# A planned attention kernel: each output store placed behind the landing of the last one, step lengths set from traces, places found anew

## Chip, cores and metric

One core of a Trainium2 chip. The metric is the time of one execution in microseconds (us), median over runs. The kernel before takes 1759.28 us (three runs, 1757.06 to 1759.89). A kernel counts as faster or slower from 2% on. Runs of one call share a chip; the chips of different calls differ, so each experiment below is compared with runs of the kernel before in the same call.

## The reference

A layer of graph attention on 16 batches of 1024 rows of 512 numbers, 8 heads of 64, with one sparse adjacency matrix for all batches:

```python
h = jnp.maximum(_layernorm(x, axis=-1), 0.0)
q, k, v = h @ Wq + bq, h @ Wk + bk, h @ Wv + bv          # in 8 heads of 64
scores = jnp.einsum('bihd,bjhd->bhij', q, k) / jnp.sqrt(64)
scores = scores + mask                                    # -1e9 where adj == 0
weights = softmax(scores); out = jnp.einsum('bhij,bjhd->bihd', weights, v)
return x + out
```

## The kernel before

Rows are sorted by their number of neighbours into 8 tiles of 128. For each tile, GpSimd gathers keys and values of the neighbours, VectorE multiplies with the queries and sums (`multiply`, `score`), ScalarE takes exponents and weighs (`exponent`, `weigh_s`), VectorE and GpSimd add up (`fold`, `join`), GpSimd adds x and stores the rows (`residual`, `put_out`). A batch has 14 such units, and a number behind a step (multiply 12, score 12) is that of its unit in the batch. TensorE meanwhile transposes normalized rows (`flip`), projects keys and values one batch ahead and queries of this batch, and adds up the weighed pieces of some units (`add_up`). For rows with many neighbours it also passes on the sums of their weights (`pass_on`, on the tile `p_more`), which needs a sum from VectorE (`more`). Before the transposes a tile's rows are normalized: VectorE takes statistics (`stats`, `variance`), GpSimd a power (`power`), VectorE a shift (`shift`), and ScalarE applies them (`norm`).

The order of the steps is not written by hand. A planner simulates five engines with a length, a place (priority) and dependences for each step, and each engine then runs its steps strictly in the order that comes out:

```python
def add(self, key, engine, length, place, after=(), uses=(), delay=0.15, moves=0.0):
    self.number[key] = len(self.ops)
    self.ops.append((key, engine, length, place, after, uses, delay, moves))
# ...
add(("residual", b, home), "POOL", 1.42, i + 2.49, [("scale", b, home)], [o, ("x", n)])
add(("put_out", b, home), "POOL", 1.5, i + 0.07, [("residual", b, home)], [("x", n)], delay=4.0, moves=0.75)
# ...
POOLS = dict(x=14, h=2, pht=2, hT=11, pkv=2, kvt=3, q=2, q0=1, g=6, acc=2, o=1)
# ...
def put_out(b, t):
    nc.gpsimd.indirect_dma_start(out=out_rows, out_offset=on(ap=perm[:, t : t + 1], axis=0),
                                 in_=X.pop(b * NT + NT - 1 - t)[:], in_offset=None, element_offset=b * N * D)
```

On the chip a store always waits until the last one has landed, since both write the same tensor. The planner of before does not know that.

## Time and profile before

| | before |
|---|---|
| median of 3 | 1759.28 us |
| profiled execution, span | 1752.1 us |
| TensorE busy / waits | 1618.9 / 122.5 us |
| GpSimd waits for the landing of a store | 37.2 us |

(The waits are the sums of all rows of the waits by engine.) The prediction shows the main views. Two more are needed to see where the time went. The first cuts the execution into start, twelve steady batches, and end. The cuts are the mark F of the prediction (end of TensorE's wait before the transposes of tiles 0/1 of the batch after next) of the first and the last steady batch. Columns: stretch, length, busy time of PE, PEld, DVE, ACT, POOL with counts, granted clock, DMA share, GB/s.

```profile
0.00:301.04 301.04, 264.57 (x740) 125.92 (x740) 251.56 (x446) 215.06 (x714) 214.10 (x219) 0.98 0.76 272
301.04:1546.97 1245.93, 1177.77 (x3121) 546.87 (x3121) 1127.26 (x1285) 1113.74 (x4213) 975.85 (x889) 0.98 0.88 314
1546.97:1752.10 205.13, 176.52 (x436) 79.01 (x436) 179.72 (x193) 160.33 (x631) 140.96 (x129) 0.92 0.77 285
```

The second is VectorE in order of time from multiply 12 on to the mark F at 1235.78 (start, duration, line, operation):

```profile
1229.55 2.29 DVE L876 TENSOR_TENSOR g<-g,pq 128x2048 f32<-128x2048 f32 x1
...
1232.95 0.68 DVE L913 TENSOR_TENSOR g<-g,g 128x512 f32<-128x512 f32 x1
1233.65 1.23 DVE L615 SCALAR_TENSOR_TENSOR shift<-mv,rstd 128x2 f32<-128x2 f32 x1
```

These are multiply 12, then (variance and fold 10 left out) join 9 and the shift that the norms and with them TensorE's transposes wait for. From the start of multiply 12 to F it is 6.23 us. The shift takes 1.23 us for two numbers a row: a GpSimd addition (1233.61, 1.25 us) runs beside it, and without one the shift takes 0.15; that will matter.

### The profile page before, as it was taken

The numbers are of one execution on the slowest core, as the hardware profiler recorded it, in microseconds if no ns is written. First come the engines' busy times: TensorE is split into PE (matmuls) and PEld (weight loads), VectorE is DVE, ScalarE is ACT, GpSimd is POOL, SyncE is SP. The second block draws the span as 40 slices with busy tenths as digits, with TensorE's granted clock in tenths as the row PEclk, the third lists the DMA queues.
The fourth block names the chain that finished last, engine by engine and source line by source line (L and its number), as shares of the span: only waits on it lengthen the run. The fifth ranks groups of instructions, "written<-read, shape, count | busy, mean of one in ns | idle before, by whom it ended". The sixth has DMA issues, their size and how long they took to land.

```text
span 1752.1 us, 19712 instructions
## 1 busy us (share of the span) xinstructions
PE 1618.9 (92%) x4295; PEld 751.8 (43%) x4295; DVE 1558.5 (89%) x1922; ACT 1489.1 (85%) x5556; POOL 1330.9 (76%) x1235
## 2 busy tenths in 40 slices
PE   6979898999999999999999999999999999999796
PEld 3444444444444444444444444444444444444333
DVE  5788989899898979989898998989989898988897
ACT  5359989898898988889898888989899898889965
POOL 4757778787787868877787877878787787877774
PEclk9989999999999999999999999999999999999989
DMA  5388889888898988988898888989988898888894
GB/s 219 132 321 293 309 292 344 309 324 316 287 329 304 339 298 309 323 284 327 305 350 303 304 304 293 346 318 328 322 294 313 293 346 304 318 311 290 310 359 169
DMA packets 150742, 531.73 MB, mean 303 GB/s; under 512 B 19916, under 2 KB 19916, under 8 KB 150616
## 3 DMA queue, kind: packets, MB, share of 16 engines
q0 software_dynamic: 109840, 390.70, 62.5%
q1 hardware_dynamic: 40776, 139.71, 21.7%
q8 instruction: 36, 0.59, 0.1%
q14 instruction: 90, 0.74, 0.1%
HBM read 429.51 MB, written 100.82 MB: 303 GB/s over the span
## 4 chain that ended last, share of the span: by engine, by line
PE 45%; DVE 18%; POOL 8%; ACT 6%; issue 4%; DMA 3%; POOLq 0%; DVEq 0%
PE pq L642 15%; PE pk L642 12%; PE pv L642 8%; DVE g L876 5%; ACT g L902 4%; PE acc L925 4%; DVE g L907 3%; DVE weights L880 3%; PE pht L632 3%; POOL g L866 3%; DVE shift L615 3%; DMA out_dram<-x,perm 2%; POOL x L966 2%; POOL g L907 1%; DVE g L896 1%
## 5 line engine op out<-in xcount | busy, mean ns | idle before, releaser
L902 ACT ACTIVATE g<-g,weights 128x64 f32<-128x64 f32 x4768 | 1180.3, 340 | 3.2 <-DVE weights L889 2.2
L866 POOL DMA_INDIRECT g<-kv,index x608 | 626.1, 1030 | 204.6 <-issue 143.5
L876 DVE TENSOR_TENSOR g<-g,pq 128x1536 f32<-128x1536 f32 (+2 forms) x208 | 389.1, 1872 | 95.4 <-PE pq L642 90.9
L642 PE MATMUL pq<-wq,hT 128*128 128x512 f32 x1024 | 460.3, 592 | 0.0
L642 PE MATMUL pk<-wk,hT 128*128 128x512 f32 x960 | 439.0, 601 | 1.8 <-ACT hT L637 1.7
L642 PE MATMUL pv<-wv,hT 128*128 128x512 f32 x960 | 431.6, 592 | 0.0
L880 DVE TENSOR_REDUCE weights<-g 128x32 f32<-128x2048 f32 (+2 forms) x224 | 423.2, 1890 | 0.6
L907 DVE TENSOR_TENSOR g<-g 128x512 f32<-128x512 f32 (+1 forms) x271 | 281.1, 1038 | 21.9 <-ACT g L902 19.8
L642 PEld LDWEIGHTS pq<-wq,hT 128*128 128x128 f32 x1024 | 194.7, 190 | 228.0 <-issue 224.7
L642 PEld LDWEIGHTS pk<-wk,hT 128*128 128x128 f32 x960 | 185.8, 194 | 212.9 <-issue 206.0
L642 PEld LDWEIGHTS pv<-wv,hT 128*128 128x128 f32 x960 | 182.5, 190 | 205.3 <-issue 201.9
L969 POOL DMA_INDIRECT out_dram<-x,perm x128 | 148.1, 1157 | 79.2 <-DMA out_dram<-x,perm 34.2
L625 ACT ACTIVATE h<-x,shift,rstd 128x512 f32<-128x512 f32 x120 | 91.3, 809 | 91.5 <-DVE shift L615 91.5
L590 POOL DMA_INDIRECT x<-in_x_dram,perm x128 | 135.9, 1062 | 34.9 <-issue 32.4
L907 POOL TENSOR_TENSOR g<-g 128x512 f32<-128x512 f32 x120 | 153.5, 1279 | 10.7 <-DVE g L907 7.2
L632 PE MATMUL pht<-ident,h 128*128 128x128 f32 x512 | 86.2, 308 | 80.2 <-ACT h L625 78.2
L632 PEld LDWEIGHTS pht<-ident,h 128*128 128x128 f32 x512 | 68.3, 158 | 139.5 <-ACT h L625 104.5
L896 DVE TENSOR_TENSOR g<-g,weights 128x512 f32<-128x512 f32 (+1 forms) x134 | 114.5, 855 | 2.2 <-ACT weights L884 1.7
L653 ACT COPY kvt<-pv 128x512 f32<-128x512 f32 x120 | 69.2, 577 | 43.0 <-PE pv L642 43.0
L966 POOL TENSOR_TENSOR x<-x,o 128x512 f32<-128x512 f32 x67 | 86.3, 1288 | 25.0 <-DVE o L957 22.1
L925 PE MATMUL acc<-g,ident 128*128 128x512 f32 x170 | 95.6, 682 | 2.8 <-POOL g L907 2.8
L637 ACT COPY hT<-pht 128x512 f32<-128x512 f32 x128 | 72.1, 575 | 26.9 <-PE pht L632 26.9
(231 smaller groups left out, 1187.0 us busy)
## 6 DMA issues: line engine op xcount, KB each, us to landing
g<-kv SPq DMA_DIRECT2D x128, 512.0 KB
kv<-kvt SPq DMA_DIRECT2D x120, 512.0 KB
g<-kv,index POOLq DMA_INDIRECT x608, 7.2
adj<-in_adj_dram SPq DMA_DIRECT2D x8, 512.0 KB
x_first<-in_x_dram SPq DMA_DIRECT2D x8, 256.0 KB
x<-in_x_dram,perm POOLq DMA_INDIRECT x128, 4.6
out_dram<-x,perm POOLq DMA_INDIRECT x128, 5.0
wk<-in_L_gnn_Wk_dram SPq DMA_DIRECT2D x1, 1024.0 KB
```

Source lines behind the costliest of these rows:

```text
L590: nc.gpsimd.indirect_dma_start(out=X[n][:], out_offset=None, in_=x_rows, in_offset=on(ap=perm[:, t : t + 1], axis=0), element_offset=b * N * D
L632: nc.tensor.transpose(PH[n][:, c, :], hn[:, ts(c, P)], ident)
L642: nc.tensor.matmul(pt, HT[n][:, c, :], W[name][:, c, :], start=False, stop=(c == DC - 1))
L866: nc.gpsimd.indirect_dma_start(out=G[i][:, s].rearrange("p j d -> p (j d)"), out_offset=None, in_=KV[b % len(KV)][:], in_offset=on(ap=inde ...
L876: nc.vector.tensor_tensor(k, k, Q[b, t][:, None, :].to_broadcast([P, count, D]), ALU.mult)
L880: nc.vector.tensor_reduce(weights[:, w, :], heads(G[i][:, :count, 0, :]), AX.X, ALU.add)
L896: nc.vector.tensor_tensor(v, v, own.to_broadcast([P, n, H, HD]), ALU.mult)
L902: nc.scalar.activation(v[:, h, :], v[:, h, :], AF.Identity, scale=weights[:, c + s, h : h + 1])
L907: engine.tensor_tensor(v[:, 0:n], v[:, 0:n], v[:, first : first + n], ALU.add)
L925: nc.tensor.matmul(ACC[b, home], owner_t if t < 0 else ident, v[:, s, :], start=(u == parts_of(home)[0] and s == 0), stop=(u == parts_of(h ...
L966: (nc.vector if shares_in(b, B, t) and b == B - 1 else nc.gpsimd).tensor_tensor(rows, rows, add, ALU.add)
L969: nc.gpsimd.indirect_dma_start(out=out_rows, out_offset=on(ap=perm[:, t : t + 1], axis=0), in_=X.pop(b * NT + NT - 1 - t)[:], in_offset=No ...
```

## The change

The intent: tell the planner that a store lands before the next can start, correct the lengths to what traces show, and search the places again. The core of the diff (some 60 lines of lengths and places, all of this kind, cut):

```diff
-        add(("rank_of", t), ("DVE", "ACT")[t >= NT // 2], 1.25, (-47.51, -44.58)[t >= NT // 2], rows("key"))
+        add(("rank_of", t), ("DVE", "ACT")[t >= NT // 2], 1.25, (-51.98, -50.40)[t >= NT // 2], rows("key"))
 ...
-        add(("tell", t), "POOL", 1.3, -35.76 + 0.3 * t, [("ranks",), ("shift", (t - NT) // 2)] + behind("tell"), delay=2.0)
-        add(("spread", t), "POOL", 1.3, -28.64 + t, [("list_of", t)] + behind("spread"), delay=2.0)
+        add(("tell", t), "POOL", 1.3, -32.06 + 0.3 * t, [("ranks",), ("shift", (t - NT) // 2)] + behind("tell"), delay=2.0)
+        add(("spread", t), "POOL", 1.3, -40.60 + t, [("list_of", t)] + behind("spread"), delay=2.0)
 ...
+    one_by_one = []
     for k in range(units):
         b, u = divmod(k, NU)
+        if b == B - 1:
+            one_by_one = []
 ...
-        add(("score", k), "DVE", 0.15 + 0.533 * count, i - -0.31, [("multiply", k)], [g])
+        add(("score", k), "DVE", 0.1 + 0.533 * count, i - -0.62, [("multiply", k)], [g])
 ...
-            add(("put_out", b, home), "POOL", 1.5, i + 0.07, [("residual", b, home)], [("x", n)], delay=4.0, moves=0.75)
+            add(("put_out", b, home), "POOL", 1.35, i + 0.07, [("residual", b, home)] + one_by_one, [("x", n)], delay=4.0, moves=0.75)
+            one_by_one = [("put_out", b, home)]
```

No arithmetic, tile or buffer changes. Only the order of each engine's steps does.

## The prediction

> **What bounds the kernel now.** I read the page's busy shares first, then the waits by engine, then the chain in order of time, and last the two stretches into which one batch falls. The kernel runs 16 batches; from the third on each engine repeats one list of instructions per batch. No share alone decides:
>
> ```profile
> PE 1618.9 (92%) x4295; PEld 751.8 (43%) x4295; DVE 1558.5 (89%) x1922; ACT 1489.1 (85%) x5556; POOL 1330.9 (76%) x1235
> ...
> DMA  5388889888898988988898888989988898888894
> ```
>
> TensorE, VectorE, ScalarE and the DMA engines are all near nine tenths busy, so the waits must say who loses time. In the time order of TensorE's instructions, only two waits come back in every batch, both in front of transposes of normalized rows:
>
> ```profile
> 1235.78 1.97 PE L632 MATMUL pht<-ident,h 128*128 128x128 f32 x8 [3.96 <-ACT h L625]
> ...
> 1287.81 0.66 PE L632 MATMUL pht<-ident,h 128*128 128x128 f32 x4 [1.33 <-ACT h L625]
> ```
>
> The first is before the transposes of tiles 0 and 1 of the batch after next (I call its end F), the second before those of tile 4. Over 13 batches the second wait averages 1.71 us (1.08 to 2.80). So I cut a batch at these two points and asked for each engine's busy time:
>
> ```profile
> 1132.94:1185.20 52.26, 50.91 (x134) 23.91 (x134) 44.62 (x59) 43.43 (x166) 40.94 (x38) 0.97 0.83 297
> 1185.20:1235.78 50.58, 46.62 (x126) 21.50 (x126) 49.15 (x50) 49.34 (x187) 40.60 (x38) 0.99 0.93 338
> ```
>
> Columns: stretch, its length, busy time of PE, PEld, DVE, ACT, POOL, granted clock, DMA share, GB/s. The first half is TensorE's: 50.9 of 52.3 us. The second half is VectorE's and ScalarE's: 49.15 and 49.34 of 50.58. The first half varies (51.9 to 55.1, mean 53.0 over 13); the second is 50.56 to 50.59 in ten of twelve, 52.1 in two. A batch is 103.8 us, from 12 batches between 301.0 and 1547.0.
>
> The wait that the change is named for is on GpSimd's queue:
>
> ```profile
> POOL out_dram L969 <- DMA out_dram<-x,perm: 34.2, 11, 4.3
> ...
> 1161.48 1.01 POOL L969 DMA_INDIRECT out_dram<-x,perm  x1 [0.17 <-POOL x L966]
> 1162.79 0.97 POOL L866 DMA_INDIRECT g<-kv,index  x1 [0.30 <-issue]
> 1164.06 0.95 POOL L866 DMA_INDIRECT g<-kv,index  x1 [0.30 <-issue]
> 1167.88 1.00 POOL L969 DMA_INDIRECT out_dram<-x,perm  x1 [2.87 <-DMA out_dram<-x,perm]
> ```
>
> (The first line is the waits by engine: total, times, longest; the rest is GpSimd in time order.) Once per batch the store of tile 7 stands two gathers behind the store of the previous batch's tile 0 and waits for it to land, 6.4 us after it was issued. It holds everything behind it. The other seven stores are far enough apart.
>
> **What the Trainium skill says.** "DMA: Bandwidth & Descriptors", section "Two DMAs through the same engine are not ordered", says only the completion semaphore orders two transfers, so the issuing engine must wait for it. The trace agrees that this wait is built in already: the stores write one tensor, and the second waits for the first's landing. The change therefore adds no wait to the machine, only to the plan. "SBUF — State Buffer", "Who interferes with whom", says a DVE instruction with two SBUF inputs contends with a GpSimd instruction that reads SBUF. The trace agrees: a 128x512 fold of VectorE takes 0.68 us alone and 2.40 us beside GpSimd's 1.28 us addition. "TensorE: Matmul & The Clock Gate", "What's actually happening", gives a halved clock after an idle window of about 3.4 us. The trace agrees: after the 3.96 us wait the granted clock is 0.61 for 3.7 us, then 1.00.
>
> **The change part by part.** The arithmetic, the tiles and the buffers stay. The planner gets one more dependence (store after landing of the last store), truer lengths, and new places; so what changes is each engine's order. Comparing the built orders of one steady batch:
>
> GpSimd. One load of x moves into the place between the two gathers and the store of tile 7. It takes 0.98 + 0.30 = 1.3 us that was waited before, so the wait falls from about 3 to about 1.7 us. The load was formerly after the store, so GpSimd gains 1.3 us per batch.
>
> TensorE, first half (F to tile 4). The sum of the last pieces (one pair of 128x512 matmuls, 0.86 us) and the small pass-on (0.12 us) move in front of the first wait, where TensorE is idle. Two query projections of tiles 7 and 6 come first, the keys of tile 0 later. What is left between F and tile 4: transposes 1.97, twelve projections at 3.65 (0.22 + 3.43 in the chain), three sums at 0.86, two transposes at 0.44: 1.97 + 43.8 + 2.6 + 0.9 = 49.2 us. The same sum for the old order gives 50.7, and 1287.81 - 1.33 - 1235.78 = 50.70 was measured, so the counting holds. The slow clock after the wait now falls on a projection: some 1.7 us at half speed, 0.85 lost, gives 50.05; other clock losses add 0.6 (mean of 13 is 51.3 against 50.7). So 50.7.
>
> Does anything hold tile 4's transposes then? They need tile 4's norm, it needs the shift on VectorE, that the power on GpSimd. On the old path this was GpSimd's chain, store wait included: power at 1283.69, F + 47.9. Now the last sums and hence the gathers and stores behind them come some 2.8 us earlier (third sum at F + 18 instead of F + 21), plus the 1.3: power near F + 44. VectorE reaches the shift near F + 47, since it waits for queries of tiles 5, 4 and 3 (ends near F + 22.8, 26.9, 38.3, plus the clock's 0.85). So the 1.71 us wait vanishes and the first half falls from 53.0 to 50.7: -2.3 us.
>
> Second half. Between the multiply of tile 2 and the shift of the batch after next, the old VectorE list has 42 steps of the plan, the new one the same 42 and three more: a 128x2048 score (2.19 us from start to start), a scale (0.60) and the sum of the pieces' weights (0.13): +2.9 us. VectorE had only 1.1 us of waits there, for ScalarE. ScalarE likewise gets one more weighing of eight 128x64 instructions (1.92) and one exponent (0.12): +2.0. Both were full, so this does lengthen the half. I choose 2.9 less the 1.1 of waits, taken to be absorbed: +1.8 us.
>
> Per batch: -2.3 + 1.8 = -0.5; for 13 batches -6.5 us.
>
> Start. Building the slot lists (88.5 to 92.4, 3.9 us) moves from VectorE's solid stretch 74 to 103 into its waits of 2.84 and 5.39 us for permutation and long rows: -3.9. Statistics of three more tiles (0.85 each) come earlier, +2.5, but leave later; the scatters of permutation data are mixed with the lists' scatters and come up to 3 us later, hidden mostly by the 5.39. TensorE waits for ranks earlier and ends the first eight tiles later, using up its 7.77 us wait. Net -2.
>
> Tail. One fold on GpSimd (1664.62, ready about 1653.4 when VectorE's fold ended) moves ahead of nine gathers. TensorE's 5.89 us wait on it goes, but VectorE, 92.9% busy from 1600 to 1700, sets the pace: -3.
>
> Sum: -11.5 us of 1759.3, so 1748.
>
> **The rivals.** First, the store wait was all of it: 34.2 us over 11 batches and some 9 more under other names. If removing it moved the end by that much, some 40 us would go, 1719. For it: it lies on the chain in several batches. Against: 1.7 us of it stays, and the second half is unmoved by it. Second, the second half takes the full 2.9 and the slow clock or VectorE's waits eat the first half's gain: then 0 to +1 per batch, 1754 to 1770. For it: 97% busy of two engines and a DMA share of 0.93. Third, VectorE's stretched instructions change with the neighbours on GpSimd. In the second half its fold, weighing and shift lose near 4.4 us (2.40 for 0.68, 1.78 for 0.68, 1.75 for 1.22, 1.23 for 0.15). If the new order avoids half, -2.2 per batch more, 1719; if it adds as much, 1777. I cannot see this from an order and set it at nothing.
>
> **Range and chances.** A microsecond per batch is 13 us; I give the halves' difference an error of about 1 us and start and tail together 5 us: 1730 to 1765 for 8 in 10. Faster by over 2% needs 1724 or less, 2.7 us per batch: 0.08. Slower by over 2% (1794.5) needs +2.7 where I have -0.5: 0.02.
>
> **What would show it.** Right: cut at the same two transposes, the first half near 50.7 with no wait before tile 4; the second near 52.6; the wait before tiles 0 and 1 at 4 to 5 us, still on ScalarE's norm; VectorE waiting over 3 us for queries in the first half; store waits near 1.7 us each. Wrong: the wait before tile 4 stays (then GpSimd's chain was not shortened), or the second half stays near 50.6 (then what I call full was not), or a new wait on gathers shows in VectorE.

## The result

The changed kernel takes 1772.24 us (four runs, 1768.43 to 1774.40); in the same rounds the kernel before takes 1759.07. The ratio is 1.0074 with an interval of 1.0055 to 1.0094: within 2%, but slower, and above the predicted range of 1730 to 1765. (A ratio is the mean time of one kernel's fast runs over that of the other's of the same rounds, so it is not quite the ratio of the medians quoted.) A repetition on another chip gave 1769.98 against 1757.08, ratio 1.0075.

The page's busy times of the changed kernel:

```profile
PE 1633.0 (92%) x4232; PEld 763.3 (43%) x4295; DVE 1556.6 (88%) x1922; ACT 1493.1 (84%) x5556; POOL 1348.5 (76%) x1235
```

VectorE and ScalarE do what they did; TensorE is busy 14.1 us longer. (63 of its records, all of small matmuls that add a bias, are missing from this trace; loads of weights show all 4295, so the number of matmuls is the same.)

The stretches cut as above:

```profile
0.00:310.65 310.65, 268.08 (x734) 129.98 (x743) 252.69 (x449) 217.36 (x723) 217.59 (x221) 0.96 0.75 267
310.65:1562.27 1251.62, 1188.24 (x3073) 554.00 (x3121) 1126.59 (x1285) 1117.41 (x4213) 992.05 (x888) 0.96 0.88 312
1562.27:1770.50 208.23, 176.69 (x426) 79.32 (x432) 177.34 (x190) 158.31 (x622) 138.88 (x126) 0.91 0.76 277
```

The start grew by 9.6 us, the twelve batches by 5.7 (104.30 us each instead of 103.83), the end by 3.1; the spans differ by 18.4. The profiled execution of before took 1753.89 us, less than its four timed runs, so this is more than the 13 us between the medians. The second pair of profiles gives 5.2, 7.5 and 3.0, together 15.7.

One steady batch of the changed kernel in its two halves, second half first:

```profile
1195.45:1249.25 53.80, 48.95 (x129) 22.41 (x129) 52.69 (x53) 50.25 (x192) 43.02 (x39) 0.96 0.94 330
1249.25:1298.84 49.59, 49.48 (x128) 23.56 (x131) 39.88 (x55) 42.83 (x161) 39.17 (x35) 0.97 0.84 299
```

Over all batches, the first half fell from a mean of 53.03 us to 50.2 (49.56 to 51.07), as predicted. The second grew from a mean of 50.83 to 54.08. In it VectorE is busy 52.69 of 53.80 us, three instructions and 3.5 us more than in the 50.58 us of before; its idle time only fell from 1.4 to 1.1.

TensorE at these points:

```profile
1246.09 0.60 PE L947 MATMUL p_more<-more,owner_t 128*128 128x8 f32 x2 [4.09 <-DVE more L943]
1246.54 2.05 PE L930 MATMUL acc<-g,ident 128*128 128x512 f32 x2
1249.25 1.97 PE L637 MATMUL pht<-ident,h 128*128 128x128 f32 x8 [0.66 <-ACT h L630]
```

The transposes of tile 4, at 1298.84, have no wait any more. But pass_on (`p_more`) now waits for `more`, here 4.09 us, in every batch, ahead of add_up and the transposes. And what follows this gap at once is slow: the two matmuls of add_up take 2.05 us instead of 1.10 at full clock, eight transposes 1.97 instead of 1.04.

VectorE from multiply 12 on:

```profile
1239.10 2.27 DVE L881 TENSOR_TENSOR g<-g,pq 128x2048 f32<-128x2048 f32 x1
...
1243.24 1.94 DVE L918 TENSOR_TENSOR g<-g,g 128x512 f32<-128x512 f32 x1
1245.10 0.15 DVE L613 TENSOR_SCALAR rstd<-mv 128x2 f32<-128x2 f32 x1
1245.21 0.69 DVE L962 TENSOR_TENSOR o<-g,inv 128x512 f32<-128x512 f32 x1
1245.82 0.21 DVE L943 TENSOR_REDUCE more<-weights 128x8 f32<-128x40 f32 x1
1245.95 2.28 DVE L885 TENSOR_REDUCE weights<-g 128x32 f32<-128x2048 f32 x1
1248.15 0.15 DVE L620 SCALAR_TENSOR_TENSOR shift<-mv,rstd 128x2 f32<-128x2 f32 x1
```

Fold 10 and the statistics of tile 1 are left out at the dots. From multiply 12 to F it is now 10.15 us instead of 6.23: 3.92 more, and the stretch ahead of multiply 12 is 0.7 shorter (43.65 against 44.35). The 3.92, counted from start to start: score 12 2.20, scale 0.61, `more` 0.13, the statistics of tile 1 0.81 (before, they stood ahead of multiply 12), join 9 1.16 more since it now runs beside GpSimd (1.86 against 0.70), the shift 1.09 less since it no longer does (0.06 against 1.15). That is 3.82; small differences make the other 0.1. The statistics only moved within the half: their 0.81 is given back in the 0.7 ahead of multiply 12. What lengthened the half is thus mostly the three added steps, 2.94 us.

GpSimd's waits for the landing of a store:

```profile
POOL x L595 <- DMA out_dram<-x,perm: 27.4, 13, 2.9
...
POOL out_dram L974 <- DMA out_dram<-x,perm: 4.2, 2, 2.6
```

The load of x that moved ahead of the store waits for the very landing that the store waited for: with 14 buffers for x it needs the one that this store frees. All rows for this landing sum to 32.2 us, 37.2 before (33.3 and 30.2 in the second pair). The wait was renamed, not filled.

### The profile page after: what moved, and what is told of

Same layout as the page of the kernel before. It is cut to its first block, busy times and chain, and to the rows that moved or that the text cites. A ratio compares the mean times of both kernels' runs of the same rounds, so it can differ in the third digit from the quotient of the medians.

```text
span 1770.5 us, 19619 instructions
## 1 busy us (share of the span) xinstructions
PE 1633.0 (92%) x4232; PEld 763.3 (43%) x4295; DVE 1556.6 (88%) x1922; ACT 1493.1 (84%) x5556; POOL 1348.5 (76%) x1235
## 4 chain that ended last, share of the span: by engine, by line
PE 47%; DVE 32%; issue 8%; POOL 5%; DMA 4%; ACT 3%; SPq 0%; DVEq 0%; POOLq 0%; ACTq 0%
PE pq L647 19%; PE pk L647 10%; PE pv L647 9%; DVE weights L885 9%; DVE g L881 8%; DVE g L912 6%; PE acc L930 4%; POOL g L871 3%; DMA g<-kv,index 3%; PE pht L637 3%; DVE g L918 2%; ACT g L907 2%; DVE st L604 1%; PE pq L645 1%; DVE g L901 1%
## 5 line engine op out<-in xcount | busy, mean ns | idle before, releaser
L871 POOL DMA_INDIRECT g<-kv,index x608 | 639.0, 1051 | 199.3 <-issue 162.2
L647 PE MATMUL pq<-wq,hT 128*128 128x512 f32 x1024 | 474.4, 607 | 0.2
L647 PE MATMUL pk<-wk,hT 128*128 128x512 f32 x960 | 431.6, 592 | 1.4
L647 PEld LDWEIGHTS pq<-wq,hT 128*128 128x128 f32 x1024 | 202.5, 198 | 229.5 <-issue 224.2
L647 PEld LDWEIGHTS pv<-wv,hT 128*128 128x128 f32 x960 | 182.6, 190 | 209.4 <-issue 206.1
L595 POOL DMA_INDIRECT x<-in_x_dram,perm x128 | 149.2, 1166 | 65.9 <-issue 32.2
L974 POOL DMA_INDIRECT out_dram<-x,perm x128 | 139.4, 1089 | 37.0 <-issue 16.8
L901 DVE TENSOR_TENSOR g<-g,weights 128x512 f32<-128x512 f32 (+1 forms) x134 | 153.9, 1157 | 0.5 <-ACT weights L889 0.5
L658 ACT COPY kvt<-pk 128x512 f32<-128x512 f32 x120 | 69.2, 577 | 71.6 <-PE pk L647 67.6
L889 ACT ACTIVATE weights<-weights 128x32 f32<-128x32 f32 (+2 forms) x224 | 49.4, 220 | 87.2 <-DVE weights L885 86.9
L930 PE MATMUL acc<-g,ident 128*128 128x512 f32 x170 | 101.6, 718 | 17.7 <-POOL g L912 15.1
L637 PEld LDWEIGHTS pht<-ident,h 128*128 128x128 f32 x512 | 70.7, 161 | 67.2 <-ACT h L630 32.2
L637 PE MATMUL pht<-ident,h 128*128 128x128 f32 x512 | 83.5, 309 | 10.5 <-ACT h L630 9.5
```

Source lines behind the costliest of these rows:

```text
L595: nc.gpsimd.indirect_dma_start(out=X[n][:], out_offset=None, in_=x_rows, in_offset=on(ap=perm[:, t : t + 1], axis=0), element_offset=b * N * D
L637: nc.tensor.transpose(PH[n][:, c, :], hn[:, ts(c, P)], ident)
L647: nc.tensor.matmul(pt, HT[n][:, c, :], W[name][:, c, :], start=False, stop=(c == DC - 1))
L871: nc.gpsimd.indirect_dma_start(out=G[i][:, s].rearrange("p j d -> p (j d)"), out_offset=None, in_=KV[b % len(KV)][:], in_offset=on(ap=inde ...
L901: nc.vector.tensor_tensor(v, v, own.to_broadcast([P, n, H, HD]), ALU.mult)
L930: nc.tensor.matmul(ACC[b, home], owner_t if t < 0 else ident, v[:, s, :], start=(u == parts_of(home)[0] and s == 0), stop=(u == parts_of(h ...
```

## The experiments

Eighteen runs in five calls. In the first and the fourth call the kernel before took 1806 and 1792 us instead of 1754 to 1759. All eight profiles of these two calls show waits that no work on the core ends, and none of the other twelve profiles does. The largest such row, from `dep_only`, on the queue of direct transfers (total, times, longest):

```profile
SPq L670 <- remote: 47.2, 3, 17.7
```

So times of these two calls are compared within the call only and with care; the form of their traces is used. What such waits are, and whether it is the chip or something else at work at that time, stays open.

In all edits that place single steps, the finished order is edited by a function `moved`, with `put(step, before= or after=)`.

### The two parts of the change, each alone

`dep_only` is the kernel before with the dependence (the lines with `one_by_one` above), old lengths and places. `no_dep` is the changed kernel without it:

```diff
-            add(("put_out", b, home), "POOL", 1.35, i + 0.07, [("residual", b, home)] + one_by_one, [("x", n)], delay=4.0, moves=0.75)
+            add(("put_out", b, home), "POOL", 1.35, i + 0.07, [("residual", b, home)], [("x", n)], delay=4.0, moves=0.75)
```

> The kernel before with only the new dependence of each output store on the landing of the last one; old lengths and places. Its plan comes out anew: the start keeps its old order (shift -4 ahead of all degree steps), but in each batch score 12 and scale 1 now stand in DVE's order ahead of the shift of tiles 0/1. Theory (what costs is what lies ahead of the shifts): first transposes on TensorE at about 15 us as before, the wait before the transposes of tiles 0/1 later by 2 to 3 us a batch, 1755 to 1790 us, start to the first such wait within 2 us of before's 301.0. Rival (the dependence itself costs or gains, through the order in which stores and loads of x reach the queue): GpSimd's waits for the landing of a store fall by more than half from 69 us in all, and the time falls to 1720 to 1750.

> The changed kernel without the new dependence: only lengths and places. Shift -4 still stands behind degree 2 at the start, and score 12 and scale 1 still ahead of the shift of tiles 0/1. Theory (lengths and places lose it): start to the first wait before transposes of tiles 0/1 still near 310 us, second halves near 54 us, 1765 to 1780 us. Rival (the dependence is what loses): back to 1750 to 1762 us, second halves near 51 us.

On the chip with waits from outside: `dep_only` 1899.75 us, `no_dep` 1808.85, before 1806.29, ratios 1.0532 and 1.0021. Both were run again on a quiet chip:

> The kernel before with the new dependence alone, a second time. Theory (an order of steps made for old lengths, in which TensorE waits 140 us for transposes, is bad on any chip): 1870 us or more again, whatever the kernel before takes. Rival (its 5.3% were due to that chip): below 1800 us on a chip where the kernel before takes 1757.

> The changed kernel without the new dependence, a second time, for a chip on which the kernel before takes 1757 us. If the lengths and places lose the time: 1768 to 1780 us as the changed kernel. If the dependence loses it: 1750 to 1762 us. On a chip where the kernel before takes 1800 or more: within 0.5% of it, as the first time.

There before takes 1754.06, `dep_only_again` 1781.51 (ratio 1.0143, 1.0106 to 1.0180), `no_dep_again` 1795.85 (1.0242, 1.0224 to 1.0260). My expectation of 1870 or more was wrong, and the rival right: most of that loss came with that call's chip. GpSimd's waits for landings at the stores, first without the dependence, then with it alone:

```profile
POOL out_dram L974 <- DMA out_dram<-x,perm: 58.1, 12, 6.5
```

```profile
POOL out_dram L974 <- DMA out_dram<-x,perm: 2.5, 1, 2.5
```

The dependence does what it is meant to do: alone it brings the waits for landings from 30 to 37 us to 12.5 (all rows). (The "69 us in all" of the expectation is in no view; the rows sum to 37.2.) The time still rises by 27 us. The whole order comes out anew, with 22.1 us of waits of GpSimd for keys and values to land that were not there, and TensorE's waits at 143 us instead of 122 to 124; which of this makes the 27 us was not tested. The new lengths and places alone bring the stores so close together that GpSimd waits 63 us (all rows), and cost 42 us. On top of them the dependence gains 26 to 29 (2.42% down to 0.75%). So each part alone is worse than both together, and the waits for landings do not by themselves tell the time: of the variants below the two fastest on quiet chips, `warm_full` and `best_full`, have 54.0 and 49.5 us of them. Lengths and places were not tried apart.

### The second half: score 12 behind the shift

```diff
+    for b in range(1, B - 1):
+        m = 4 * (b + 2)
+        if ("shift", m) in order:
+            put(("score", b * NU + 12), after=("shift", m))
+            put(("exponent", b * NU + 12), after=("norm", 2 * m + 1))
```

> The changed kernel with score 12 of each steady batch put behind the shift of tiles 0/1 on DVE, and its exponent behind the norms on ScalarE. Theory (2.2 us of the score lie on the path that ends TensorE's wait): second halves 54.1 to about 52, 1742 to 1750 us. Rival (`more` on TensorE and the folds behind keep the wait where it is, or the halves trade): second halves fall by less than 0.7 us or the first halves grow by as much, 1765 to 1774 us.

In the disturbed call: 1765.97 us. Against `start` of the same call (below), whose batches are the changed kernel's, the twelve batches take 1243.5 us instead of 1254.7, under one us each. Second halves have a mean of 53.55 instead of 54.05: half a microsecond was gained there, so the rival was right about the halves (its time cannot be judged in this call). The first halves gained 0.4 as well; the section on the clock says what went with it. VectorE shows where the other 1.7 us of the score's 2.2 went:

```profile
1243.91 0.22 DVE L958 TENSOR_REDUCE more<-weights 128x8 f32<-128x40 f32 x1
1244.61 1.23 DVE L635 SCALAR_TENSOR_TENSOR shift<-mv,rstd 128x2 f32<-128x2 f32 x1 [0.49 <-POOL rstd L631]
```

Without the score in between, the shift arrives 0.49 us before GpSimd's power is done, and then runs beside GpSimd's next addition: 1.23 us instead of 0.15. From the start of `more` to the start of what follows the shift it is 1.85 us, against 2.39 in the changed kernel. The score had filled a wait and avoided a collision. In the sum for the second half it costs 0.54 us, not 2.2.

Then pass_on was moved as well:

```diff
+            put(("pass_on", b), after=("flip", 2 * m + 1))     # added to the edit above
```

> The changed kernel with score 12 behind the shift of tiles 0/1 (as in the second-half experiment before, which gained 0.5 us a second half) and also pass_on behind the transposes of tiles 0/1 on TensorE, so that TensorE no longer waits for `more` ahead of them. Theory (there the wait on `more` took the place of the wait on the score; 1.5 us more a batch come with it, and with one gap of TensorE fewer its slow stretch after a gap is shorter by some 0.5 us): second halves 51 to 52.5 us, time 25 to 35 us below the changed kernel. Rival (the second half is bound by VectorE's whole list of steps, 98% busy, and by gathers that land late, so each wait removed shows up elsewhere): less than 12 us below the changed kernel.

1764.85 us, ratio 1.0062 (1.0045 to 1.0079), the twelve batches 1248.45 us (104.04 each). Against the changed kernel's 1.0075 the gain is about 2 us and lies inside the intervals; the theory's 25 to 35 us are refuted. The 56.8 us of waits on `more` (`after_again`) are gone, and 53.8 on folds and 32.1 on norms (14.8 and 10.3 in `after_again`) stand in their place.

### The chain of tiles 0/1 earlier

```diff
+        k = b * NU + 11                                        # for each steady batch
+        put(("stats", n + 1), after=("multiply", k))
+        put(("variance", n // 2), after=("stats", n + 1))
+        put(("power", n // 2), after=("gather", k + 2, 2))
+        put(("shift", n // 2), before=("multiply", k + 1))
+        put(("norm", n), after=("weigh_s", k, 0))
+        put(("norm", n + 1), after=("norm", n))
+        put(("flip", n), before=("pass_on", b))
+        put(("flip", n + 1), before=("pass_on", b))
+        put(("pass_on", b), after=("add_up", k - 1))
```

> The changed kernel with, in each steady batch, the chain of tiles 0/1 of the batch after next made earlier: statistics, variance and shift ahead of multiply 12 on DVE, the power ahead of fold 9 on GpSimd, the norms behind the first product of unit 11 on ScalarE, and the transposes ahead of add_up 10 and pass_on on TensorE. Theory (TensorE's idle 4 to 5 us there are only the wait for these steps; DVE's surplus of the second half can be worked off in the first half, in which it idles 10 of 50 us): 2.5 to 3.5 us less a batch, 1772 to 1730 to 1742 us. Rival (DVE's work is what ends every second half; what is taken away there comes back as waits of TensorE for queries' buffers or for add_up): less than 1 us a batch, 1760 to 1775.

1778.27 us at the median, spread over 1768.54 to 1783.73, ratio 1.0106 (1.0073 to 1.0139). Not a microsecond was gained; the rival is right and even too kind. The halves trade: the mark F comes earlier and second halves take 48.8 to 51.7 us, but what stood ahead of it, add_up and pass_on among it, now stands in the first halves, which take 54.2 to 58.0. TensorE waits 42.9 us for folds and 52.6 for norms.

### The start and the tail

TensorE's first transposes start at 14.92 us before and at 21.52 changed. The first shift stands behind three degree steps on VectorE, which wait for the adjacency matrix. It looks like a loss of 6.6 us. Put back in its place:

```diff
+    put(("shift", -4), before=("degree", 0))
```

> The changed kernel with shift -4 put ahead of degree 0 on DVE, nothing else. Theory: the first transposes start near 15 us instead of 21.5, and since TensorE is busy from there on, the first wait before transposes of tiles 0/1 moves from 310.7 to 303 to 306 us, and the whole from 1772 to about 1766. Rival (the start is bound by the list of edges or by loads further on, so the early transposes only wait later): first transposes at 15 us, but the first such wait still near 310 us and the time 1770 to 1774.

The first transposes began at 16.7 us, the mark F at 312.0, in the disturbed call (1777.62 us). `score` of the same call, which has the changed start, has F at 314.9, and quiet profiles of that start have it at 306.3 to 310.7. So a gain is not shown, and one of 2 us or so is not excluded. Next, all steps ahead of the first multiply in the order of before:

```diff
+    order[: len(START)] = START        # the same steps, sorted as in the plan before
```

> The changed kernel with all steps ahead of the first multiply in the order that they had in the plan before. Theory (the start's 9.6 us come from the steps that make the list of edges, the tell scatters above all): the first wait before transposes of tiles 0/1 moves from about 311 to 300 to 304 us, the whole shorter than the changed kernel by 7 to 11 us. Rival (the loss lies behind the first multiply): less than 3 us.

1772.57 us, ratio 1.0090: nothing gained. TensorE's step that needs the list of edges (`p_before`) began as early as before (103.40 us; 103.37 before, 111.74 changed, 109.54 in the changed kernel of the same call), and then, on TensorE:

```profile
115.66 0.59 PE L693 MATMUL pq<-bq_parts,chosen 128*128 128x512 bf16 x1 [8.11 <-DVE g L929]
```

At the seam, where the old order ends and the new one goes on, VectorE waits 5.69 us for a load of x that the new order asks for earlier than the old one issues it, and TensorE waits 8.11 us behind it: the 6 us gained on the list were lost here. So the seam was moved back by one batch:

> The changed kernel with all steps up to the third batch's first transposes (the mark from which steady batches are counted) in the order of the plan before. With only the steps ahead of the first multiply put back, TensorE gained 7 us at the list of edges and lost 8.1 us at once at the seam, waiting for a multiply on VectorE that stood behind a late load of x. Theory (the 9.6 us of the start are order alone): that mark at 300 to 304 us instead of 310.7, the time 6 to 10 us below the changed kernel. Rival: the gain is lost again behind the seam, less than 3 us.

(The seam is at the first transposes of tile 0 of batch 2, one batch ahead of the mark F; my expectation took the two for the same.) The fourth call was disturbed: the mark came at 312.6, the time was 1776.20 against 1792.21 of before. A cleaner answer is in the last pair below, which share a quiet chip: with the old start the seam is reached at 200.1 us instead of 203.8, and the mark F at 305.8 instead of 308.1. So order accounts for some 2 to 4 us. The profiles on quiet chips that share the changed kernel's start and whose edits lie behind it or hardly reach it put the mark at 306.3, 306.4, 308.1, 308.2 and 310.7; the two of before at 301.0 and 303.0. The 9.6 us of the first pair are thus 5.9 us between the means, of which 2 to 4 are shown to be order. The rest is open.

The tail:

```diff
+    k = (B - 2) * NU
+    put(("fold", k + 11, 1, 1), before=("gather", k + 26, 2))
+    put(("put_out", B - 2, 1), after=("gather", k + 24, 1))
+    put(("fold", k + 13, 2, 1), after=("multiply", k + 24))
+    put(("add_up", k + 11), after=("fold", k + 11, 1, 1))
```

> The changed kernel with four steps of the last part as the kernel before has them: fold 207 on GpSimd behind the first gathers of unit 222 instead of ahead of all gathers of unit 220, the store of tile 1 of the last batch but one behind the first of these gathers, fold 209 on DVE behind multiply 220, add_up 207 on TensorE behind its fold. Theory (the gathers of the last batch issued 2.9 us late and DVE's wait of 5.0 us behind it make the tail longer): 3 to 6 us less. Rival (the tail is bound by TensorE's and DVE's work further on): within 1 us.

1768.81 us, ratio 1.0087 (1.0061 to 1.0113): by the clock no gain. From the last F to the end the profile has 206.1 us, against 207.4 to 208.8 in five quiet profiles with the unchanged tail and 205.1 and 204.6 before. So some 2 of the 3 us, too little for these intervals.

### The chips

> The kernel before, unchanged, profiled on the same chip as the next three. On the chip of the first four experiments it took 1806 us at the median of 23 runs instead of 1759, while the changed kernel with one step moved took 1778 there. Theory (that chip lands stores later, and the kernel before issues its stores close behind one another): on such a chip the batches of this run vary between 102 and 112 us, with GpSimd's waits for the landing of a store near 60 us in all instead of 34; on a chip like the first one the time is 1757 to 1760. Rival (granted clock or the engines differ): the batches are all longer alike, with a lower clock or longer instructions.

> The changed kernel, unchanged, on the same chip. Theory: it takes 1768 to 1780 us on any chip, with batches of 104 us, whatever the kernel before takes there. Rival: it is slower by the same share as the kernel before.

1755.48 and 1769.98 us, on a quiet chip. The result repeats. Why the kernel before lost more (1806 us) in the first call than `start` (1778) or `score` (1766), which contain the new order, cannot be said: no execution of before was profiled there. My theory of later landings has no support, since `no_dep` there waits for landings 65.4 us and on the quiet chip 63.0.

### TensorE's clock behind its gap

In the twelve batches TensorE is busy 10.5 us longer with the same matmuls, while its waits fell only from 68.1 to 60.8 us. Dummy work, which the real transposes overwrite, can close the gap:

```diff
+        def warm(n):
+            PH[n] = ps_h.tile([P, DC, P], F32, tag="pht", name=f"pht_{b}_{t}")
+            for _ in range(24):
+                nc.tensor.transpose(PH[n][:, 0, :], ident, ident)
 ...
+            order.insert(order.index(("proj_kv", n - 1, 1)) + 1, ("warm", n))
```

> The changed kernel with 24 transposes of the identity, which nobody reads (they are overwritten by the real ones), on TensorE right behind the last projection of each steady batch, in the place of the first part of its wait for `more`. At full clock they take about 2.6 us of the 4.0 to 5.9 us wait. Theory (the changed kernel's TensorE is busy 14 us longer than before with the same matmuls, since the sum, transposes and query projections that follow its gap run at half clock): pq's mean falls from 607 to 592 to 596 ns, TensorE's work without the dummies by 12 us or more, and the time by 8 to 16 us. Rival (VectorE's list ends the second half anyway and the faster matmuls only wait longer later): pq's mean falls, waits of TensorE grow by as much, the time within 4 us of the changed kernel.

> The same 24 transposes in the kernel before, ahead of the transposes of tiles 0/1. Theory: pk's mean falls from 601 to about 592 ns, the transposes behind the gap from 1.97 to 1.04 us, and the time by 8 to 16 us, to 1741 to 1749 on a chip where the kernel before takes 1757. Rival: within 4 us of the kernel before.

1783.76 and 1786.97 us against 1792.21 (disturbed call); ratios 0.9949 and 0.9975. The test failed in its aim: pq's mean is 612 ns, and in `warm_before` pk's mean rose from 601 to 606 ns instead of falling to 592. TensorE in one batch of `warm_after`, behind the 24 dummies:

```profile
1049.50 0.39 PE L972 MATMUL p_more<-more,owner_t 128*128 128x8 f32 x2 [1.52 <-DVE more L968]
1049.74 1.10 PE L955 MATMUL acc<-g,ident 128*128 128x512 f32 x2
1052.66 1.97 PE L655 MATMUL pht<-ident,h 128*128 128x128 f32 x8 [1.81 <-ACT h L647]
```

Two idle pieces of 1.52 and 1.81 us with 1.3 us of work between them were enough for the slow stretch. The granted clock shows how. Two stretches of 3.41 us, in the columns of above (TensorE busy 1.35 and 2.87 us; the granted clock is the third number from the end):

```profile
1048.71:1052.12 3.41, 1.35 (x4) 0.52 (x4) 3.41 (x5) 1.26 (x6) 3.09 (x3) 1.00 1.00 297
1052.12:1055.53 3.41, 2.87 (x10) 2.38 (x11) 3.41 (x4) 3.41 (x11) 2.80 (x3) 0.50 0.99 353
```

In all 20 profiles the clock is either full or half. (The 0.61 of the prediction is a mean over 3.7 us, most of them at half.) But for the last one of each profile, which the end cuts off, every slow stretch has a length of 3.41 us or a multiple of it. All 381 of them start right behind 3.41 us in which TensorE was busy for at most 0.51 of the time. Cut the same way, the full clock has over 9000 stretches that no slow one follows; none of them was busy for less than 0.41. A slow stretch ended only behind 3.41 us that were busy for 0.76 or more. So what counts is the share of work in a piece of 3.41 us, and one long wait is not needed; work that comes in small pieces behind a gap keeps the clock low for longer. In the twelve batches the slow time is 58 us before and 101 changed: one stretch of 3.4 us behind most gaps before, 6.8 or 10.2 behind each gap of the changed kernel. `score` has 83 where `start` has 104, which fits its gain in the first halves; in `score_pass` it is 98 again. `warm_after` has 69, and `warm_before` 31 where the kernel before has 58.

So both pieces were filled:

```diff
+            order.insert(order.index(("proj_kv", n - 1, 1)) + 1, ("warm", n, 36))
+            order.insert(order.index(("flip", n)), ("warm", n, 14))
```

> The changed kernel with its gap of TensorE filled as far as it goes: 36 dummy transposes behind the last projection and 14 more between add_up and the real transposes. With 24 in one piece, gaps of 1.5 and 1.8 us were left and the slow stretch still came. Theory (the slow clock costs the 10.5 us): pq's mean falls to 592 to 598 ns, TensorE's work without dummies to about 1620, and the steady batch from 104.3 to about 103.3 us. Rival (VectorE's list ends the half): pq's mean falls as well, but the batch stays at 104.0 to 104.6 us, since TensorE only reaches its waits sooner.

1759.01 us (22 runs) against 1755.13 (39 runs): ratio 1.0018 (1.0008 to 1.0027), where the changed kernel has 1.0074 and 1.0075. That is 10 us less. The same place:

```profile
1127.25 4.09 PE L661 MATMUL pht<-ident 128*128 128x128 f32 x36
1132.08 0.39 PE L971 MATMUL p_more<-more,owner_t 128*128 128x8 f32 x2 [0.73 <-DVE more L967]
1132.33 1.10 PE L954 MATMUL acc<-g,ident 128*128 128x512 f32 x2
1133.27 1.69 PE L661 MATMUL pht<-ident 128*128 128x128 f32 x14
1135.24 1.36 PE L653 MATMUL pht<-ident,h 128*128 128x128 f32 x8 [0.28 <-ACT h L645]
1136.44 0.38 PE L669 MATMUL pq<-bq_parts,chosen 128*128 128x512 bf16 x1
1136.65 3.60 PE L671 MATMUL pq<-wq,hT 128*128 128x512 f32 x8
```

The first eight matmuls of pq take 3.60 us; pq's mean is 594 ns instead of 607. The twelve batches, of which 3.4 us are slow:

```profile
308.14:1550.84 1242.70, 1223.93 (x3673) 600.23 (x3721) 1139.18 (x1285) 1114.01 (x4213) 987.88 (x888) 1.00 0.89 315
```

They take 103.56 us each instead of 104.30. First halves fall from 50.2 to 49.05, second halves grow from 54.1 to 54.5. The theory holds: without the slow clock the half that TensorE bounds is 1.2 us shorter, and the half that VectorE bounds gains nothing. Dummy transposes count as work for the clock.

### All together

Old start up to the seam, score 12 and pass_on behind, the tail's four steps, and dummies. First with 24 dummies in one piece, then with 26 ahead of add_up and 22 ahead of the transposes (these are the edits shown above, in one function):

> All that helped or should help together in the changed kernel: the start's old order up to the mark, score 12 and pass_on behind the shift and the transposes, the tail's four steps as before, and the 24 dummy transposes. If the gains add up (9 + 5 to 8 + 1 to 3 + 8 to 16): 1735 to 1748 us, faster than both kernels on a chip where the kernel before takes 1757. If the batch is bound by VectorE's list: 1752 to 1762.

> All that helped together, with dummies before the sum and before the transposes: the start's old order up to the mark, score 12 and pass_on behind, the tail's four steps, 26 and 22 dummies. On a chip where the kernel before takes 1757 with no waits ended from outside: 1740 to 1755 if the gains add up (1 batch = 103.0), 1755 to 1765 if VectorE's list ends the halves. On a chip with such waits: below the kernel before in any case, by 1% or so.

`best`: 1773.81 against 1792.21, ratio 0.9900, in the disturbed call, with the slow stretch still there; not comparable with quiet chips. `best_full`: 1749.06 (18 runs) against 1755.13, ratio 0.9967 (0.9957 to 0.9978), on a quiet chip: faster than both kernels, by 0.3% and some 1%, clear of noise but within the 2%. Against `warm_full` of the same call its span is 13.7 us shorter: 2.3 at the start, 8.2 in twelve batches (102.87 each), 3.2 at the end. The 0.7 us a batch lie in the second halves (a mean of 53.8 instead of 54.5). The moves of score and pass_on alone had shortened second halves by 0.6 too (`score_pass`, 53.4), while first halves kept their slow clock and grew to 50.6. So these moves are the likely cause; that it is not the other split of dummies was not tested apart.

## Why the prediction was wrong

The sum of -11.5 us stands against +18.4 and +15.7 in the spans of the two pairs. Of the difference, 12 to 13 us are the batches, 7 to 12 the start and 6 the tail. Of the prediction's signs some came true (first halves near 50.7 without the wait before tile 4; VectorE waits 3.7 us for queries there), others did not (second halves at 54.1 and not 52.6; the wait for the norms is 0.66 and not 4 to 5, since `more` is waited for ahead of it).

- **First half, -2.3 us: right.** -2.8 was measured; the wait before tile 4's transposes is gone. Its 49.2 us at full clock are right, since `warm_full` measured 49.05; the slow clock costs some 1.2 and not 0.85 and 0.6.
- **Second half, "2.9 less the 1.1 of waits, taken to be absorbed: +1.8": the step that failed in the batches.** It measured +3.25, which makes the batch 0.47 us longer instead of 0.5 shorter: some 12 us of difference over the batches. The three added steps cost 2.94 as counted. But waits did not absorb 1.1 of it: VectorE's idle time fell by 0.3 only (1.43 to 1.11), and its other steps took 0.6 longer. The contention that rival three "set at nothing" gave join 1.16 more and the shift 1.09 less, next to nothing in sum. The experiment with the score shows that a step's length is not its cost either: taken out, its 2.2 us gained 0.54.
- **Start, -2: wrong in sign.** The slot lists' 3.9 us did not shorten the path: TensorE's step that needs the list of edges began 8.4 us later (111.74 instead of 103.37), and its wait ahead of it, said to be used up, was 5.60 instead of 7.77. F came 9.6 later in the first pair, 5.9 between means; 2 to 4 us of it are order, the rest is open. Putting the first shift back was tested in the disturbed call only and shows no clear gain; putting back all steps ahead of the first multiply, scatters among them, gained nothing.
- **Tail, -3: wrong in sign,** +3.1 from the last F, although the first half inside it gained as predicted. Four steps put back give some 2 of it in the profile and nothing that timing could resolve. That VectorE sets the pace there was right; that its order would improve was not.
- **"One load of x moves into the place ... that was waited before": wrong.** The load needs the buffer that the waited-for store frees. The wait changed its name. The first half gained without it.
- **"Where TensorE is idle": half right.** Add_up and pass_on moved into the gap, but pass_on brought its own wait, for `more`. Moving it away gained about 2 us at most, since folds and norms wait next.
- **What was not in the sum at all:** TensorE's gap makes the work after it slow, and filling it is worth 0.7 to 0.8 us a batch. The prediction carried this as a fixed loss, though its own order broke the gap into pieces, with which the slow time rose from 58 to 101 us.

Of the rivals the second (1754 to 1770) came closest. The first speaks of "some 9 more under other names"; the rows show 3.0. It is refuted by `dep_only_again`, where the time rises with most of the waits for landings gone, and by `best_full`, where it falls with 49.5 us of them (37.2 before).

## What to carry to other kernels

Before counting on a step that "fills" a wait, ask what buffer it needs and who frees it. Where two engines take turns at being the bound, a step moved out of one half can come back in the other, as in `early`; the largest single gain here came from what is truly saved, the slow matmuls behind a gap, and dummy work of the idle engine saved them. A better dependence in a planner changes every order; test it together with the lengths and places it was tuned with, and each part alone, before reading a gain or a loss into it.

## What the Trainium skill lacked or had wrong

- "TensorE: Matmul & The Clock Gate", section "What's actually happening", ties the half clock to an idle window of about 3.4 us. The length agrees (3.41), but here the window need not be idle: behind 3.41 us busy for less than 0.41 of the time the half clock always came, behind more than 0.51 never, and the page gives no such share. Idle pieces of 1.52 and 1.81 us with 1.3 us of work between brought it (eight transposes 1.97 us), 0.73 and 0.28 us did not (1.36 us, and the next projections at 3.60). The page does not say that filler work can hold the clock in the middle of a kernel: 50 transposes of about 0.11 us in each gap saved 10 of 1770 us.
- "SBUF — State Buffer", section "Who interferes with whom", has the rule that fits (two SBUF inputs on VectorE beside a GpSimd read), but no time for such a pair. Here the shift takes 1.23 us beside GpSimd and 0.15 without, the join of 128x512 1.94 and 0.68.
- No page has that the same program takes longer on some chips: the kernel before took 1754 to 1759 us in four calls and 1792 and 1806 in two, and all profiles of those two calls show 2 to 36 waits that no work on the core ends, which the others do not.
